# A third set of edges fetched row by row, by SyncE: a graph layer on one core

## The chip, the cores and the metric

The kernel runs on one core of a Trainium2 chip. A core has TensorE (PE, matrix products), VectorE (DVE), ScalarE (ACT), GpSimd (POOL) and SyncE (SP, which only issues transfers and waits). SP, ACT and POOL can issue transfers (DMAs) between HBM and the core's memory. The metric is the device time of one launch in microseconds (us), as the median of several runs.

## What is computed

The reference is one layer of a graph network on 50000 nodes of 160 features (64 scalars s and 32 vectors v of three components), with 1650000 edges sorted by their destination: 800000 random ones, the same turned round, and one from each node to itself. Each edge has four numbers e0 and e1 (three components).

```
ss, vv = s[src], v[src]
dot    = einsum('eui,ei->eu', vv, e1)
out0   = C0 * (ss*e0 @ W1 + dot*INV3 @ W2)
p3     = (ss @ W3)[:, :, None] * e1[:, None, :] * INV3
p4     = einsum('eui,uw->ewi', vv*e0, W4) * INV3
p5     = einsum('eui,uw->ewi', cross(vv, e1), W5) * INV6
m      = concat(out0, C1 * (p3 + p4 + p5))
m_agg  = segment_sum(m, dst)
h      = m_agg through Ws and Wv
out    = layernorm(x + x + relu(h))
```

All of it is linear in x[src] for given edge numbers. So the kernel first adds up x[src] times each of the four edge numbers over the edges of a destination (160 x 4 sums a node), and applies the products of the weights once per node.

## The kernel before, in words

**Units, pairs, stages.** The edges are worked in units of 128: one unit is one matmul `ps += ha.T @ xg` at line 502. `xg` holds the source rows of its 128 edges (128 x 160 f32); `ha` says, for four edge numbers and a window of 32 destination nodes, what each edge adds where. Six units make a group, two groups a pair (12 units, one PSUM tile `ps`), ten pairs a stage (120 units). There are some 104 stages. The loop over pairs begins at line 1002; in it a matmul is issued for each unit, and between them the program puts the other work: turning the sums and adding them into a ring of node sums (lines 518 and 527), making the next pair's `ha` (lines 474 and 477), blocks of 128 nodes finished by PE (line 822), DVE (lines 185 to 201) and ACT (line 195), their residual rows loaded (`xt`, line 765) and results sent (line 920).

**Where source rows come from.** GpSimd fetches most units with one indirect DMA each (`gather`, line 459), into a pool of four `xg` tiles of a pair each; so it can be up to four pairs ahead of PE. Two units in each stage of 120 are fetched otherwise: DVE makes a list of byte offsets (`list_rows`, lines 403 and 404), and ACT loads 32 of them at a time into registers (line 372) and issues one DMA of 640 bytes for each edge (line 376, 128 for a unit), into tiles `xscalar`. These rows have semaphores of their own; the matmul that reads the tile waits for the full count (line 505). That is the class `Fetcher` (line 351). The set of fetched units of a stage s is asked for from pair 4 of stage s - 1 to pair 4 of stage s, evenly by unit (`deal`, line 388): with two sets, one in the first half of this and one in the second. They stand at units 38 and 98 of the stage (line 357). Fetching runs in all stages but the first ones and the last ones (line 1026).

**SyncE's queue** carries, in the order of the program: the edges of the stage after next (`r`, `fd`, lines 270 and 276), the residual rows, the node rows and shares for a new part of the ring (`xr`, `sa`, line 798), the sends, and the packing. Packing takes the self edges out: in eleven packs of 128 rows of edges, DVE and ACT shift the edges together (lines 604 to 706) in a tile `prow`, and SyncE writes each row back with two DMAs (`store` and `put`, lines 715 to 740: one of 28 KB, one of 0.8 KB), 16 in a batch after one load of offsets (line 722), 17 batches in a pack. The next pack's first ACT operation (line 604) overwrites `prow` and waits for these stores.

**Order.** SP, PE, DVE and ACT run in the order in which the program writes their instructions (line 1000). Work of nodes is queued as tasks and worked off one step per unit (`work`, line 872); steps of a pack are spread evenly up to their due pair (line 1032). A send waits for DVE's result `o` (line 201); the residual rows of a block are waited for by DVE's `hot` (`lands`, line 466).

Of the kernel before, what the change touches and what calls it, by code (L numbers as in the profile page):

```python
# [77 lines left out]
KM = WS - 1  # L78
REST = 15
LEAD = 3  # L80
BY_SCALAR, BY_SYNC = 2, 0
FBEGIN, FWAIT = 4, 4

def plan(n_nodes, n_edges):
# [1132 lines left out]
```

## Time and profile before

| | us |
|---|---|
| median of 3 runs | 15476.25 (15474.15 to 15478.85) |
| profiled execution, its own time | 15480.47 |
| its span, first to last instruction | 15478.7 |

The profile shows one further execution. In its views PE, DVE, ACT and POOL are the engines; PEld is the loading of a matmul's weights; SPq, ACTq and POOLq are the queues of instructions that issue or wait, whose time is not counted as busy. `out<-in` names the tiles that an instruction writes and reads, L459 is a line of the kernel, x12 a count. "idle before, releaser" is the time in which an engine did nothing ahead of an instruction, and what ended it; "issue" means that it waited for nothing the profile shows. In a view of one line or tile the three numbers are the shortest, median and longest duration in ns, then first and last start.

### The profile page before, as it was taken

What the parts mean: (1) busy time and instruction counts of PE and PEld (TensorE: products, weight loads), DVE (VectorE), ACT (ScalarE), POOL (GpSimd) and SP (SyncE); (2) the same over time, 40 slices, a digit from 0 to 9 for tenths busy, and PEclk for the clock granted to TensorE, in tenths of its full rate; (3) what the DMA queues carried; (4) which work ended last, traced back from release to release, by engine and by line L of the source; (5) the groups of instructions that cost most, each with busy time, mean ns of one, the idle gap of its engine ahead of it and who ended that gap; (6) DMA issues with size and microseconds to landing.
All of it is one profiled execution on the core that took longest, in us unless ns stands there. A gap on an engine that the chain in (4) does not pass through costs nothing.

```text
span 15478.7 us, 148655 instructions
## 1 busy us (share of the span) xinstructions
PE 10475.4 (68%) x28971; PEld 6817.4 (44%) x28972; DVE 7640.9 (49%) x12532; ACT 171.6 (1%) x273; POOL 11680.1 (75%) x12331
## 2 busy tenths in 40 slices
PE   3466766667666666766666666667666666766666
PEld 3344444444444444444444444444444444444444
DVE  8455355445535543563455355445534553554333
ACT  0000000000000000000000000000000000000000
POOL 7777777777777777777777777777777777777777
PEclk6655555555555555555555555555555555555555
DMA  3333333333333333333333333333333333333333
GB/s 83 96 84 95 89 81 84 100 86 80 92 93 81 82 97 89 80 85 100 84 81 93 92 81 83 99 87 80 85 100 84 81 89 90 80 86 85 83 81 75
DMA packets 887906, 1345.20 MB, mean 87 GB/s; under 512 B 281438, under 2 KB 660450, under 8 KB 884310
## 3 DMA queue, kind: packets, MB, share of 16 engines
q0 software_dynamic: 591264, 1009.88, 27.6%
q1 hardware_dynamic: 242218, 308.07, 6.2%
q10 hardware_dynamic: 53488, 17.70, 0.6%
q14 instruction: 705, 5.78, 0.1%
q8 instruction: 231, 3.78, 0.1%
HBM read 1263.28 MB, written 71.42 MB: 86 GB/s over the span
## 4 chain that ended last, share of the span: by engine, by line
POOL 53%; issue 24%; DMA 16%; PE 6%; DVE 1%; POOLq 0%
POOL xg L459 53%; DMA xg<-in_x,si 16%; PE ps L502 5%; PE phb L822 1%; DVE ha L477 0%; DVE ring L527 0%; DVE sums L518 0%; DVE ring L813 0%; DVE hot L474 0%; DVE prow L688 0%; DVE xr L809 0%; DVE pri L683 0%; DVE marks L681 0%; DVE ring L524 0%; DVE ring L772 0%
## 5 line engine op out<-in xcount | busy, mean ns | idle before, releaser
L459 POOL DMA_INDIRECT xg<-in_x,si x12318 | 11676.6, 948 | 3777.4 <-issue 3517.7
L502 PE MATMUL ps<-xg,ha 128*128 128x160 f32 x24636 | 9735.6, 506 | 4990.9 <-DMA xg<-in_x,si 4453.7
L502 PEld LDWEIGHTS ps<-xg,ha 128*128 128x128 f32 x24636 | 5828.3, 293 | 8646.9 <-DMA xg<-in_x,si 7413.5
L518 DVE STREAM_TRANSPOSE sums<-ps 128x320 f32<-128x320 f32 x1044 | 535.5, 513 | 6834.6 <-PE ps L502 6820.7
L477 DVE TENSOR_TENSOR ha<-hot,pk 128x1536 f32<-128x1536 f32 x1044 | 1829.7, 1753 | 35.8
L822 PE MATMUL phb<-BWk,ring 128*128 128x160 f32 (+1 forms) x3910 | 1289.8, 428 | 0.0
L822 PEld LDWEIGHTS phb<-BWk,ring 128*128 128x128 f32 (+1 forms) x3910 | 1058.1, 304 | 0.1
L527 DVE TENSOR_TENSOR ring<-ring,sums 128x160 f32 x2087 | 683.1, 327 | 329.3 <-issue 190.7
L474 DVE TENSOR_TENSOR hot<-bank,rel 128x384 f32<-128x384 f32 x1044 | 572.4, 548 | 44.2 <-DMA xt<-in_x 42.4
L688 DVE COPY_PREDICATED prow<-marks,prow 128x2370 f32<-128x2370 int32 (+5 forms) x198 | 548.5, 2770 | 1.1
L813 DVE STREAM_TRANSPOSE ring<-xr 128x1280 f32<-128x1280 f32 x188 | 469.0, 2495 | 6.5
L688 DVE COPY_PREDICATED pra<-marks,pra 128x1580 f32<-128x1580 int32 (+5 forms) x198 | 377.0, 1904 | 0.0
L809 DVE TENSOR_TENSOR xr<-xr,bank 128x1280 f32<-128x1280 f32 x188 | 278.8, 1483 | 6.6 <-DVE bank L808 0.2
L185 DVE SCALAR_TENSOR_TENSOR y<-phb,xt 128x320 f32<-128x320 f32 x196 | 95.6, 488 | 308.7 <-PE phb L822 308.2
L195 ACT ACTIVATE rstd<-mv,eps_t 128x2 f32<-128x2 f32 x196 | 58.0, 296 | 14063.1 <-DVE mv L190 13240.1
L524 DVE TENSOR_TENSOR ring<-ring 128x196 f32<-128x196 f32 (+20 forms) x485 | 148.9, 372 | 1.8
L502 PE MATMUL ps<-xscalar,ha 128*128 128x160 f32 x408 | 146.8, 462 | 0.0
L201 DVE TENSOR_SCALAR o<-y,mv,rstd 128x160 f32<-128x160 f32 x391 | 131.7, 378 | 7.5
L685 DVE COPY_PREDICATED_SCALAR hit<-marks,none 128x395 int32 (+5 forms) x198 | 129.8, 655 | 7.0
L772 DVE MEMSET ring<- 128x1280 f32 (+1 forms) x98 | 119.3, 1218 | 22.6 <-issue 22.6
L189 DVE BATCH_NORM_STATS2 st<-y 128x6 f32<-128x160 f32 x391 | 121.6, 311 | 6.7
L686 DVE COPY_PREDICATED hit<-marks,pri 128x395 int32<-128x395 int32 (+5 forms) x198 | 118.1, 597 | 6.9
(351 smaller groups left out, 2061.2 us busy)
## 6 DMA issues: line engine op xcount, KB each, us to landing
xscalar<-in_x ACTq DMA_DIRECT2D x26112, 0.6 KB
xg<-in_x,si POOLq DMA_INDIRECT x12318
xr<-in_x SPq DMA_DIRECT2D x187, 640.0 KB
r<-edges SPq DMA_DIRECT2D x100, 384.0 KB
edges<-prow SPq DMA_DIRECT2D x1330, 27.8 KB
xt<-in_x SPq DMA_DIRECT2D x195, 160.0 KB
out<-o SPq DMA_DIRECT2D x195, 160.0 KB
pra<-in_attr SPq DMA_DIRECT2D x10, 2370.0 KB
```

The lines of the kernel that those rows point to most:

```text
L201: nc.vector.tensor_scalar(o[:n, i], y[:n, i], mv[:n, i, 0:1], rstd[:n, i:i + 1], op0=ALU.subtract, op1=ALU.mult)
L459: nc.gpsimd.indirect_dma_start(out=xg[:, j, :], out_offset=None, in_=x, in_offset=bass.IndirectOffsetOnAxis(ap=placed[0][:, u + j:u + j + ...
L474: idle[:] = [nc.vector.tensor_tensor(hot[:, :n], slotsP[:, 0:W].unsqueeze(1).to_broadcast([P, n, W]), rel[:, u:u + n].unsqueeze(2).to_broa ...
L477: nc.vector.tensor_tensor(ha[:, :n], hot[:, :n].unsqueeze(2).to_broadcast([P, n, NK, W]), pk[:, :, u:u + n].rearrange("p k u -> p u k").un ...
L502: mm = nc.tensor.matmul(ps[:, j // G, :], ha[:, j].rearrange("p k w -> p (k w)"), xr, start=j % G == 0, stop=j % G == G - 1)
L518: nc.vector.transpose(at[:, :ng], ps[:, :ng].rearrange("p g (b f) -> p g b f", f=FB))
L524: nc.vector.tensor_tensor(ring[k][:, b, :past], ring[k][:, b, :past], ring[k - 1][:, b, S:S + past], op=ALU.add)
L527: nc.vector.tensor_tensor(here, here, at[:, i], op=ALU.add)
L688: nc.vector.copy_predicated(what[:n, a:e], mi[:, r].unsqueeze(2).to_broadcast([n, e - a, what.shape[2]]), what[:n, a + d:e + d])
L809: nc.vector.tensor_tensor(xr[:, :nq], xr[:, :nq], sumP[:, :nq].unsqueeze(2).to_broadcast([P, nq, D]), op=ALU.mult)
L813: nc.vector.transpose(ring[k][:, :, c0:c0 + nq * W].rearrange("p b (w q) -> p q b w", q=nq), xr[:, :nq].rearrange("p q (b f) -> p q b f", ...
L822: wrote("misc", nc.tensor.matmul(ph[:nb], ring[k][:, i, c0:c0 + nb], BWk[:, i, :], start=i == 0, stop=i == ND - 1))
```

## The change

One constant: SyncE gets one set.

```
-BY_SCALAR, BY_SYNC = 2, 0
+BY_SCALAR, BY_SYNC = 2, 1
```

What follows from it in the program:

- The list of fetchers (line 394) has a second member: engine SP, a pool `sync` of two tiles (BY_SYNC + 1, line 245), eight semaphores, one set a stage. By line 357 its unit is ceil((4 + 10 + 4 - 10) x 12) + 8 = 104 of 120. Its rows are dealt over the same ten pairs, 128 in 120 units.
- SP's program gets, in each of these stages, four loads of 32 offsets and 128 DMAs of 640 bytes, in between what stands there already.
- GpSimd's program loses the gather of unit 104 in these stages: 12216 instead of 12318.
- PE's matmul of that unit reads `xsync` and waits for its semaphore.
- DVE's list is made for three units: one more operation at line 403, and 96 elements a partition instead of 64 at line 404.

## The prediction

> **What bounds the kernel now.** I read the page first: span, busy shares, the chain that ended last, the costliest groups.
>
> ```profile
> span 15478.7 us, 148655 instructions
> PE 10475.4 (68%) x28971; PEld 6817.4 (44%) x28972; DVE 7640.9 (49%) x12532; ACT 171.6 (1%) x273; POOL 11680.1 (75%) x12331
> ...
> POOL 53%; issue 24%; DMA 16%; PE 6%; DVE 1%; POOLq 0%
> ...
> L459 POOL DMA_INDIRECT xg<-in_x,si x12318 | 11676.6, 948 | 3777.4 <-issue 3517.7
> ```
>
> No engine is full, yet one explains the time. GpSimd issues 12318 gathers (line 459); their busy time and the idle time just before them are 11676.6 + 3777.4 = 15454.0 us, all of the span but 25 us. Of that idle time 3517.7 us is "issue": GpSimd waited for nothing that the profile shows. Next I asked the timeline what one gather takes, and whether anything else ever holds it up.
>
> ```profile
> 635.27 0.95 POOL L459 DMA_INDIRECT xg<-in_x,si  x1 [0.30 <-issue]
> 636.52 0.95 POOL L459 DMA_INDIRECT xg<-in_x,si  x1 [0.30 <-issue]
> ...
> 639.01 0.95 POOL L459 DMA_INDIRECT xg<-in_x,si  x1 [0.30 <-issue]
> 653.24 0.94 POOL L459 DMA_INDIRECT xg<-in_x,si  x1 [13.28 <-PE ps L502]
> 654.49 0.95 POOL L459 DMA_INDIRECT xg<-in_x,si  x1 [0.30 <-issue]
> ```
>
> A gather starts every 1.25 us: 0.95 us of work, 0.30 us between two. One real wait shows, 13.28 us at 640 us, and it matters below. Is 1.25 us a property of GpSimd, or does it give when SyncE and ScalarE issue beside it? I compared two stretches of 270 us, by busy time of line 459 (the columns: stretch, length, POOL busy, count, clock, DMA share, GB/s): one in which SyncE stores packed rows one by one while ScalarE fetches, one in which SyncE is almost quiet.
>
> ```profile
> 1410.00:1680.00 270.00, 204.46 (x216) 0.55 0.36 96
> 1740.00:2010.00 270.00, 204.21 (x216) 0.54 0.32 78
> ```
>
> 216 gathers in each, 1.25 us apiece, whatever the hardware queues do. So the kernel is bound by the number of gathers that GpSimd issues.
>
> **What the change removes.** ScalarE's fetched rows count the stages in which fetching runs. The views of its lines 376 and 372 give the register load, the issue and the load of 32 offsets (minimum, median and maximum in ns), the timeline an unbroken run of rows:
>
> ```profile
> L376 ACTq MOVE xscalar<-in_x x26112: 29/29/38, 245.2 to 15290.0; - x200
> L376 ACTq DMA_DIRECT2D xscalar<-in_x x26112: 227/228/1947, 245.3 to 15290.1; - x200
> ```
>
> ```profile
> L372 ACTq TENSOR_LOAD <-line x816: 2141/2298/6078, 242.9 to 15277.6; - x164
> ```
>
> ```profile
> 664.67 9.14 ACTq L376 DMA_DIRECT2D xscalar<-in_x  x29
> ```
>
> 26112 / 128 = 204 sets, two in a stage, so 102 stages; SyncE gets one set in each, the same condition. GpSimd loses 102 gathers: 102 x 1.25 = 127.5 us.
>
> **What it adds on SyncE.** 128 rows and four loads of offsets in a stage. The last row above has 29 rows in 9.14 us, 0.315 us each. The trace shows no such row on SyncE; its nearest row of the same kind is its own store (line 739, below), with 227 ns against 228 for the issue. So a stage adds 128 x 0.315 + 4 x 2.3 = 49.5 us of SyncE's time, and a stage lasts 118 x 1.25 = 147.5 us. What is free there? SyncE's own waits in one ordinary stage, 5000 to 5148 us:
>
> ```profile
> SPq L920 <- DVE center L321: 65.7, 1, 65.7
> SPq L920 <- DVE o L201: 61.3, 1, 61.3
> ```
>
> 127 us of 148: the rows fit into time that SyncE spends in front of line 920, the send of finished blocks. Queued behind the new wait for the list (line 372) are that engine's loads, sends and stores; but the list is asked for in the program at the pair whose DVE work makes it, where SyncE waits for the sends anyhow. The set is dealt until pair 4 of its stage (unit 48) and read at unit 104: 56 units, 70 us of slack, as with ScalarE's second set. The tile asked for was read two stages before, so its wait is nothing. PE's 102 sets of matmuls stay, with another operand. DVE gets one more operation of line 403 in a stage,
>
> ```profile
> L403 DVE TENSOR_SCALAR held<-r x198: 166/180/428, 705.6 to 15167.4; 128x32 f32<-128x32 f32 x198
> ```
>
> and a longer one at line 404; both lie in DVE's idle half (49% busy) and would be 102 x 0.18 = 18 us without that cover. Do ScalarE's rows suffer when SyncE issues beside them? In the stretch of stores from 1410 to 1680 us:
>
> ```profile
> L376 ACTq DMA_DIRECT2D xscalar<-in_x x487: 227/228/1175, 1417.6 to 1679.4; - x163
> ```
>
> The median stays at 228 ns, so I cost it at nothing; a doubled issue in all 128 rows would be 128 x 0.23 = 29 us a stage, beside 256 x 0.315 + 8 x 2.3 = 99 us of 147.5: it would still fit.
>
> **The one place without cover** is the first store of packed rows. SyncE's part, and its waits, from 407 to 628 us, then who waited from 560 to 720 us:
>
> ```profile
> L739 SPq DMA_DIRECT2D edges<-prow x136: 223/227/2102, 407.7 to 626.9; - x136
> L739 SPq DMA_DIRECT2D selves<-mine x136: 223/227/363, 408.1 to 627.3; - x136
> ```
>
> ```profile
> SPq L739 <- DMA edges<-prow: 62.7, 93, 3.0
> SPq L739 <- DMA selves<-mine: 13.4, 53, 0.3
> ```
>
> ```profile
> ACT prow L604 <- DMA edges<-prow: 122.8, 1, 122.8
> ...
> DVE hot L474 <- DMA xt<-in_x: 42.4, 1, 42.4
> ...
> POOL xg L459 <- PE ps L502: 13.9, 3, 13.3
> ```
>
> SyncE is late here. DVE waits 42.4 us for a load of nodes queued behind the stores, ScalarE 122.8 us for the stores' end, DVE for ScalarE, PE for DVE; GpSimd, up to four buffers ahead, loses the 13.28 us seen above. Any delay of the stores' end goes straight into that loss. In the changed order 101 rows and four loads of the second set stand among these 272 stores (five rows and a load just ahead of the first), five to seven rows between two batches of 16. They take 101 x 0.315 + 4 x 2.3 = 41 us of issue. Upper bound: 41 us, all added. Lower bound: 0, since SyncE waits 76 us in 146 places for its own transfers, and rows issued meanwhile cost nothing; below nothing it can't be, as nothing is taken off this queue. I take 12 us, nearer to the waits' row: a batch's rows take some 2 us of issue, against 76 / 17 = 4.5 us of waiting per batch, and are hidden; what is left is the rows' time in the transfer queue, by ScalarE's queue (packets, MB, share)
>
> ```profile
> q10 hardware_dynamic: 53488, 17.70, 0.6%
> ```
>
> 0.006 x 16 x 15478.7 / 26112 = 0.057 us a row, 101 of them 5.8 us, and some 2 us (an estimate) for each of the three loads inside the stretch, which come together with rows (2.3 + 2 us, about a batch's wait). Also, the two sets used before this wait (units 104 of stages 2 and 3) gain nothing: GpSimd merely waits 2.5 us longer. In the later ten packs the stores' end is not waited for: in the second one the last stores are issued at 1683 us and ScalarE overwrites the rows at 1875 us:
>
> ```profile
> 1683.70 0.23 SPq L739 DMA_DIRECT2D selves<-mine  x1
> ```
>
> ```profile
> 1874.80 2.30 ACT L604 CAST prow<-pri 128x1185 f32<-128x1185 int32 x1 [27.64 <-PE ps L502]
> ```
>
> 191 us of room against some tens of delay.
>
> **Sum.** -127.5 + 2.5 + 12 = -113 us. The profiled execution took 15480.47 us (1.8 around its span), so 15367.5; it lies 4.2 us over the median of the runs, so I forecast 15363 for the median.
>
> [...] The GpSimd rows above are the bound, at 1.25 us for each issue. [...]
>
> **Rivals.**
> 1. *The first pack costs more.* The 41 us are added whole, and ScalarE, catching up after it, falls up to as far behind again: -127.5 + 2.5 + 41 to twice 41, so 15392 to 15433. For it: SyncE's queue has no free time from 407 to 628 us. Against: the 76 us of waits.
> 2. *The transfer is the bound, not the issue.* If the gathers' pace came from the DMA engines, each fetched row would give its time back: 15476. For it: DMA holds 16% of the chain. Against: 216 gathers in both stretches, at 96 and 78 GB/s.
> 3. *Slower: SyncE can't issue a set in a stage.* SyncE's 147.5 us less 20 of other work and 9.2 of loads leave 118 us, 0.92 us a row; above that each stage waits for its rows. Its stores, with their waits, go at (627.3 - 407.7) / 272 = 0.81 us; at 1.0 us a row a stage takes 128 + 29 = 157 us in place of 147.5, 102 of them 970 us more: 16446. Against: the row's 0.315 us on ScalarE, three times faster than the limit.
>
> That the change doesn't do what it says is excluded: 102 gathers fewer stand in the built program, and PE reads 102 of SyncE's tiles.
>
> **How the numbers follow.** Forecast 0.79: 15363, with its own range from 15347 (nothing lost in the first pack: -127.5 + 2.5, 15351, and the 4 us by which runs scatter) to 15392. Rival 1 0.07, rival 2 0.06, rival 3 0.08. The range, 15345 to 15400, holds the forecast and the near part of rival 1. A measurement here can tell about 0.2%, 31 us. Faster: 0.79 + 0.07 = 0.86; same 0.06; slower 0.08.
>
> **What would show it.** GpSimd's count falls to 12216 and its interval stays at 1.25 us, or the sum's first term is wrong. The wait near 640 us grows from 13.3 to about 28 us (13.3 + 2.5 + 12). Line 376 on SyncE shows 13056 issues near 228 ns. PE shows no new long waits before a matmul on xsync. The forecast is wrong if the interval rises past 1.263 us (12216 x 0.0104 = 127 us), or if GpSimd waits for PE in many stages.

## The result, and the profile after

| | before | after |
|---|---|---|
| median of 15 runs of each, us | 15474.18 (15469.4 to 15479.1) | 15444.51 (15439.69 to 15449.57) |
| profiled execution, its span, us | 15478.7 | 15438.1 |

The ratio of after to before is 0.9981, with an interval of 0.9973 to 0.9989: 30 us won, 0.2%, where 113 were forecast and the range ended at 15400. The profiled execution of before lay some 6 us above its median and that of after some 4 us below its own, so the two profiles are 40.6 us apart, and the budget below has to explain those.

From the page of after: span, engines, the queue of SyncE (q1) and that of ScalarE (q10), the chain that ended last, and the group of the gathers.

```profile
span 15438.1 us, 175175 instructions
...
q1 hardware_dynamic: 268330, 316.48, 6.6%
q10 hardware_dynamic: 53488, 17.70, 0.6%
...
POOL 51%; issue 21%; DMA 19%; PE 4%; DVE 1%; SPq 0%; POOLq 0%; DVEq 0%
...
L459 POOL DMA_INDIRECT xg<-in_x,si x12216 | 11581.5, 948 | 3831.6 <-issue 3491.8
```

The count is 12216 as forecast and the mean of one is 948 ns in both kernels. But the idle time ahead of the gathers rose from 3777.4 to 3831.6 us although there are 102 fewer of them, and only part of it is "issue". What the rest is, the waits of GpSimd over the whole span say (total in us, times, longest). Before:

```profile
POOL xg L459 <- issue: 3517.7, 11532, 1.3
POOL xg L459 <- PE ps L502: 203.3, 623, 13.3
POOL xg L459 <- DMA xg<-in_x,si: 44.7, 134, 1.0
```

After:

```profile
POOL xg L459 <- issue: 3491.8, 11413, 2.0
POOL xg L459 <- PE ps L502: 185.1, 437, 33.7
POOL xg L459 <- DMA xg<-in_x,si: 140.4, 328, 1.7
```

Each gather has some 0.30 us of idle time before it anyway, whatever is named as its releaser. So each row is read by what it holds over 0.30 us a time. Waits for PE: 203.3 - 623 x 0.30 = 16.4 us before, 185.1 - 437 x 0.30 = 54.0 after, so +37.6. Waits for the transfer of an earlier gather: 44.7 - 134 x 0.30 = 4.5 before, 140.4 - 328 x 0.30 = 42.0 after, so +37.5. "Issue": 0.3050 us a time before, 0.3059 after, so 11413 x 0.0009 = some +10. With -127.5 for the gathers that went, the sum is -42 us, against 40.6 measured between the spans. Two costs are to be explained, of about 37 and 48 us.

**The first: PE's waits at the first pack.** Who waited from 560 to 760 us in after:

```profile
ACT prow L604 <- DMA edges<-prow: 142.6, 1, 142.6
...
DVE hot L474 <- DMA xt<-in_x: 68.1, 1, 68.1
PE ps L502 <- DVE ha L477: 58.1, 1, 58.1
DVE hit L625 <- ACT marks L624: 53.6, 3, 36.7
...
POOL xg L459 <- PE ps L502: 48.3, 2, 33.7
```

GpSimd's 13.3 us became 48.3, in two waits, one of 33.7 and the other of 14.6 us. DVE's wait for the nodes queued behind the stores grew by 68.1 - 42.4 = 26 us. The stores themselves, from 400 to 700 us in after:

```profile
L739 SPq DMA_DIRECT2D edges<-prow x136: 223/228/1047, 412.2 to 662.5; - x136
L739 SPq DMA_DIRECT2D selves<-mine x136: 223/228/1199, 412.5 to 662.8; - x136
```

They end at 662.8 us instead of 627.3, 35.5 us later. The busy time of the gathers up to 760 us (columns as in the prediction) shows the loss by the count. Before, then after:

```profile
0.00:760.00 760.00, 560.34 (x586) 0.66 0.35 89
```

```profile
0.00:760.00 760.00, 529.29 (x554) 0.65 0.31 85
```

32 gathers fewer, of which two were taken out: GpSimd stands 30 x 1.25 = 37.5 us behind.

**The second: gathers that come in late, everywhere.** SyncE's rows go out as fast as ScalarE's:

```profile
L376 SPq MOVE xsync<-in_x x13056: 29/29/39, 244.7 to 15225.3; - x198
L376 SPq DMA_DIRECT2D xsync<-in_x x13056: 224/228/9388, 244.7 to 15225.3; - x198
```

PE waits for none of them. But where both engines issue rows at once, as in this stretch of after (SyncE, then ScalarE),

```profile
6789.81 18.36 SPq L376 DMA_DIRECT2D xsync<-in_x  x39
```

```profile
6790.04 18.54 ACTq L376 DMA_DIRECT2D xscalar<-in_x  x49
```

GpSimd is held up for a moment, and what ends its wait is the transfer of an earlier gather:

```profile
6808.54 0.95 POOL L459 DMA_INDIRECT xg<-in_x,si  x1 [0.30 <-issue]
6810.39 0.94 POOL L459 DMA_INDIRECT xg<-in_x,si  x1 [0.91 <-DMA xg<-in_x,si]
6812.07 0.94 POOL L459 DMA_INDIRECT xg<-in_x,si  x1 [0.73 <-DMA xg<-in_x,si]
6813.72 0.94 POOL L459 DMA_INDIRECT xg<-in_x,si  x1 [0.70 <-DMA xg<-in_x,si]
```

The rows hardly slow each other's issue: each of these two runs has a load of 32 offsets of some 2.3 us in it, and from row to row ScalarE takes 0.342 us on average with a row of SyncE's within 0.4 us, and 0.345 without; SyncE takes 0.358 with one of ScalarE's and 0.355 without (steps under 1.5 us). But three gathers lose 0.61 + 0.43 + 0.40 us here.

The trace's packet records tell where. A gather is recorded as 16 packets each of 640, 4480 and 4 bytes (before, 591264 packets for 12318 gathers, 48 each) and raises its semaphore in 16 steps; a sixteenth of it, eight rows, is called a share here. A fetched row is one packet of 640 bytes and one of 4: in after SyncE's queue has 13056 more of each, for 13056 rows. In eight of the gathers from 6802 to 6818 us, one of the 16 packets of 4480 bytes took 0.75 to 1.17 us; from 6710 to 6730 us, 99 in 100 took 0.38 us or less. One share of sixteen is late, and the wait for a gather ends with its last share, as the next paragraph shows.

One late share doesn't hold GpSimd yet. The records of the semaphores (the counters that a transfer raises when it lands) show that the gathers go round eight of them, and that each waits for the one eight before it, issued some 10 us earlier. The gather at 6810.39 us started 0.26 us after the last share of that earlier gather had landed, at 6810.14; its other 15 shares had landed by 6802.36. The next two gathers show the same, 0.26 us behind a share that came over 8 us after the other 15. So a queue is worked off: the packets of the rows go on until 6816.6 us, 8 us after the last of them was issued, and GpSimd stands still here where this queue outlasts eight gathers. From 760 to 15300 us, 12 gathers before and 312 after had a last share that landed more than 7 us behind the middle one.

The same records show the order in that queue. From 6806.1 to 6816.7 us the packets of 640 and 4 bytes of SyncE's queue and of ScalarE's, and the gathers' six late ones (0.76 to 1.17 us), stand one behind the other, none overlapping the next by more than 6 ns: no row's packet runs beside a late one. No view names a transfer engine. That one engine carries a row, and that the rows of both queues and the late shares meet on the same one, is the author's inference from this place; the expectations below take it as given.

### The profile page after: what moved, and what is told of

The parts are those of the page before. It is cut to its first block, busy times and chain, and to the rows that moved or that the text cites. A ratio compares the mean times of both kernels' runs of the same rounds, so it can differ in the third digit from the quotient of the medians.

```text
span 15438.1 us, 175175 instructions
## 1 busy us (share of the span) xinstructions
PE 10171.0 (66%) x28971; PEld 6746.8 (44%) x28972; DVE 7652.8 (50%) x12634; ACT 171.5 (1%) x273; POOL 11585.0 (75%) x12229
## 4 chain that ended last, share of the span: by engine, by line
POOL 51%; issue 21%; DMA 19%; PE 4%; DVE 1%; SPq 0%; POOLq 0%; DVEq 0%
POOL xg L459 51%; DMA xg<-in_x,si 18%; PE ps L502 3%; DMA selves<-mine 1%; PE phb L822 0%; DVE ha L477 0%; SPq L739 0%; DVE prow L688 0%; DVE ring L527 0%; SPq L376 0%; DMA xt<-in_x 0%; DVE sums L518 0%; DVE hot L474 0%; DVE ring L813 0%; DVE xr L809 0%
## 5 line engine op out<-in xcount | busy, mean ns | idle before, releaser
L459 POOL DMA_INDIRECT xg<-in_x,si x12216 | 11581.5, 948 | 3831.6 <-issue 3491.8
L502 PE MATMUL ps<-xg,ha 128*128 128x160 f32 x24432 | 9418.3, 500 | 5253.2 <-DMA xg<-in_x,si 4659.5
L502 PEld LDWEIGHTS ps<-xg,ha 128*128 128x128 f32 x24432 | 5765.7, 292 | 8675.4 <-DMA xg<-in_x,si 7382.9
L822 PE MATMUL phb<-BWk,ring 128*128 128x160 f32 (+1 forms) x3910 | 1250.3, 417 | 0.0
L822 PEld LDWEIGHTS phb<-BWk,ring 128*128 128x128 f32 (+1 forms) x3910 | 1020.3, 294 | 0.0
L474 DVE TENSOR_TENSOR hot<-bank,rel 128x384 f32<-128x384 f32 x1044 | 573.1, 549 | 69.9 <-DMA xt<-in_x 68.1
```

Source lines behind the costliest of these rows:

```text
L459: nc.gpsimd.indirect_dma_start(out=xg[:, j, :], out_offset=None, in_=x, in_offset=bass.IndirectOffsetOnAxis(ap=placed[0][:, u + j:u + j + ...
L474: idle[:] = [nc.vector.tensor_tensor(hot[:, :n], slotsP[:, 0:W].unsqueeze(1).to_broadcast([P, n, W]), rel[:, u:u + n].unsqueeze(2).to_broa ...
L502: mm = nc.tensor.matmul(ps[:, j // G, :], ha[:, j].rearrange("p k w -> p (k w)"), xr, start=j % G == 0, stop=j % G == G - 1)
L822: wrote("misc", nc.tensor.matmul(ph[:nb], ring[k][:, i, c0:c0 + nb], BWk[:, i, :], start=i == 0, stop=i == ND - 1))
```

## The experiments

**Theory 1**: both costs come from the added rows, late stores in the first pack and late gathers in the rest; **theory 1a**: by their number, not their bytes. Its rivals put the loss elsewhere: into the gap that the missing gather leaves in the order of PE's pairs (A), into transfers of ScalarE and GpSimd that have moved against the stores (B), into SyncE's rows alone without ScalarE's (C), or, for the first pack, into the rows' transfers and not SyncE's time (E). D is a cost of the paced versions: loads and stores that come late. The expectations state them with their numbers.

**The first four runs** come from a chip where the kernel before itself took 20491.12 us. There ScalarE is slow, and not GpSimd the bound, so they don't answer the question.

Gathers removed (unit 104 reads a tile of zeros; these edges are left out of the sums):

```diff
-BY_SCALAR, BY_SYNC = 2, 1
+BY_SCALAR, BY_SYNC = 2, 0
@@ gather
+                if rows[j] is None and u + j == 104 and 1 < s < NSC - 1:
+                    rows[j] = nothing, None, None, None
```

> The kernel before, with the gather of unit 104 left out in the same 102 stages and nothing fetched in its place; its matmul reads a tile of zeros, so those edges are left out of the sums. Theory 1 (the interval of 1.25 us per gather is GpSimd's own): 102 x 1.25 = 127.5 us less, of which 2.5 us are lost in the first pack: 15474 - 125 = 15349, GpSimd's interval unchanged. Rival A (pairs with two fetched units wait for PE): clearly less, about half, 15400 to 15420.

Rows added (all gathers kept, SyncE's rows fetched as well):

```diff
-                if rows[j] is None:
+                kept = rows[j] is None
+                if kept:
                     rows[j] = xg[:, j, :], None, None, None
+                if kept or u + j == 104:
                     nc.gpsimd.indirect_dma_start(
```

> The changed kernel, but GpSimd gathers unit 104 as well (into its place in the gathered tile, which nothing reads), so that only the price of SyncE's rows is left, against the kernel before. The changed kernel's profile puts 38 us more than before into the first 760 us and some 48 us into gathers later on that start late, 1.5 to 2.7 us after the one before. Theory 1 (the two losses are the price of the rows, whatever GpSimd does): 15474 + 86 = 15560, from 15545 to 15575. Rival A (the late gathers come from PE or from the pairs with two fetched units, so they go when the gather is kept): only the first pack is left, 15474 + 38 = 15512.

Late start (SyncE's sets begin only after the first pack):

```diff
+FIRST = 4
@@ list_rows
-                f.prepare(s, line[:, i], at, u0 + at)
+                if f.et != ET.SP or s > FIRST:
+                    f.prepare(s, line[:, i], at, u0 + at)
@@ loop over pairs
-                        f.begin(0 < s < NSC - 2)
+                        f.begin((0 if f.et != ET.SP else FIRST - 1) < s < NSC - 2)
```

> The changed kernel, but SyncE's fetching begins three stages later, for the set of stage 5, after the first pack's stores. 99 gathers fewer than before instead of 102. Theory 1 (the first pack's loss comes from rows queued among the stores on SyncE): the stores from 412 to 663 us end near 627 again, GpSimd's wait near 640 us is back at 13.3 us, and the time is 15444 - 38 + 3.75 = 15410. Rival B (the stores end late because the transfers of ScalarE and GpSimd have moved against them): the stores still end past 650 us and the time stays near 15445.

One set each:

```diff
-BY_SCALAR, BY_SYNC = 2, 1
+BY_SCALAR, BY_SYNC = 1, 1
```

> The changed kernel with one set for ScalarE and one for SyncE instead of two and one: as many gathers (12318) and as many fetched rows as before, but from two queues. Theory 1 (gathers start late where the rows of both queues together load one transfer engine): half of ScalarE's rows are gone, so the late gathers go too, and only the first pack's loss is left: 15474 + 38 = 15512, GpSimd's waits for transfers near 4 us over its usual interval as before. Rival C (two hardware queues that issue at the same time disturb GpSimd or each other, whatever the sum of rows): the late gathers stay, 15474 + 38 + 30 to 48 = 15540 to 15560.

Measured on that chip: gathers removed 20360.39 us (ratio 0.9929, 0.9906 to 0.9952), rows added 21107.81 (1.0296, 1.027 to 1.0322), late start 20935.52 (1.0225, 1.0202 to 1.0248), one set each 19685.72 (0.961, 0.9586 to 0.9635). Waits of the first of them:

```profile
ACT rstd L195 <- issue: 18146.0, 176, 150.4
...
DVE rstd L199 <- ACT rstd L195: 6435.3, 133, 74.6
POOL xg L461 <- PE ps L506: 4027.1, 354, 46.5
```

DVE waits 6435 us for ScalarE, 4.3 us on the usual chip, and GpSimd waits for PE 4027 us. ScalarE's 22 rows in one unbroken run took 23.78 us there, 30 of them 11.99 us on the usual chip, each with one load of offsets. With ScalarE the bound, a set taken from it helps and rows added beside its own cost more. Why that chip's ScalarE was slow isn't settled. All later runs come from chips where the kernel before took 15475 to 15485 us.

**1. The gathers removed, again.**

> The kernel before, with the gather of unit 104 left out in the same 102 stages and nothing fetched in its place; its matmul reads a tile of zeros, so those edges are left out of the sums. It is run again because the first four runs came from a chip on which the kernel before took 20491 us. Where the kernel before takes some 15475 us: theory 1 (the interval of 1.25 us per gather is GpSimd's own) gives 102 x 1.25 = 127.5 us less, 2.5 us of it lost in the first pack: ratio 0.9919. Rival A (pairs with two fetched units wait for PE): clearly less, about half, ratio 0.995 to 0.997.

15363.14 us against 15484.4: ratio 0.9922 (0.9906 to 0.9939), -121 us. Waits of GpSimd:

```profile
POOL xg L461 <- PE ps L506: 198.0, 594, 17.3
POOL xg L461 <- DMA xg<-in_x,si: 46.9, 142, 1.4
```

Over the usual 0.30 us, 19.8 and 4.3 us, against before's 16.4 and 4.5. Nothing new is waited for, so A is out: the missing gather costs PE nothing. The first term of the forecast's sum holds.

**2. The rows added, again**, on top of all gathers.

> The changed kernel, but GpSimd gathers unit 104 as well (nothing reads it), so that only the price of SyncE's rows is left; run again for a chip on which the kernel before takes some 15480 us. Without the gathers and without the rows the time was 15363 against 15484, so removing is worth 121 us; the changed kernel gained 30, so the rows should cost some 91. Theory 1 (the first pack's loss and the late gathers are the price of the rows, whatever GpSimd does): 91 us more than before, ratio 1.0059. Rival A (the late gathers come with the pairs that have two fetched units, and go when the gather is kept): the first pack's 38 us alone, ratio 1.0025.

15569.51 us against 15476.57: ratio 1.0061 (1.0046 to 1.0077), +93 us. Its waits:

```profile
POOL xg L461 <- PE ps L504: 178.5, 431, 31.5
POOL xg L461 <- DMA xg<-in_x,si: 132.5, 301, 1.8
```

49.2 and 42.2 us over the usual, as in after. -121 + 93 = -28, the change's -30: the two halves add up, and the whole loss is what the rows cost.

**3. The late start, again.** It leaves SyncE's rows out of the first pack; three sets of 102 aren't fetched, so 99 x 1.25 = 124 us are to be won.

> The changed kernel, but SyncE's fetching begins three stages later, for the set of stage 5, after the first pack's stores; 99 gathers fewer than before instead of 102. Run again as above. Theory 1 (the first pack's loss comes from rows queued among the stores on SyncE): the stores end near 627 us again instead of 663, GpSimd's wait near 640 us is back at 13.3 us, and the ratio to before is 0.9981 - (38 - 3.75) / 15474 = 0.9959. Rival B (the stores end late because ScalarE's and GpSimd's transfers have moved against them): they still end past 650 us, ratio 0.998.

15406.55 us: ratio 0.9954 (0.994 to 0.9967), -70 us. Its stores from 400 to 700 us, then GpSimd's waits:

```profile
L741 SPq DMA_DIRECT2D edges<-prow x136: 223/228/2060, 406.9 to 627.1; - x136
```

```profile
POOL xg L461 <- PE ps L504: 148.5, 434, 14.1
POOL xg L461 <- DMA xg<-in_x,si: 132.5, 310, 2.7
```

The stores end at 627 us again, the longest wait for PE is 14.1 us, and 40 us of the loss are gone. B is out. The 39.5 us of late gathers stay: the two costs are separate.

**4. One set each for ScalarE and SyncE**: as many rows and gathers as before, split over two queues.

> The changed kernel with one set for ScalarE and one for SyncE instead of two and one: as many gathers (12318) and as many fetched rows as before, from two queues. Run again as above. Theory 1 (gathers start late where the rows of both queues together load one transfer engine): with half of ScalarE's rows gone the late gathers go too, and only the first pack's 38 us are left: ratio 1.0025, and GpSimd's waits for transfers come near those of before (44.7 us by the page). Rival C (rows from SyncE's queue delay the gathers whatever the sum of rows, for instance because they share it with stores and loads): the late gathers stay, 38 + 30 to 48 us: ratio 1.0044 to 1.0056, and the waits for transfers near 140 us.

15495.38 us: ratio 1.0012 (1.0003 to 1.0021), +19 us. Waits:

```profile
POOL xg L459 <- PE ps L502: 187.5, 517, 29.6
POOL xg L459 <- DMA xg<-in_x,si: 58.3, 177, 1.7
```

The late gathers are gone: 58.3 - 177 x 0.30 = 5.2 us, though SyncE fetches as many rows as in after. Last shares more than 7 us behind are 17 here, against 312 in after. So C is out: the sum of both engines' rows makes gathers late. The first pack still loses, but less than I expected: its stores end at 643.7 us, and waits for PE hold 32.4 us over the usual where after has 54.0. ScalarE's own rows there are halved.

**5. The late start, paced.** In experiment 3, SyncE has its rows issued in bursts, whenever it comes out of a wait. Here the first row after each pair's nodes waits for DVE's `hot` of that pair, which spreads them.

```diff
                     row.then_inc(sem, 16)
+                    if self.et == ET.SP and paced:
+                        tc.add_manual_dep(row.ins, paced.pop().ins.name, LANDED)
@@ loop over pairs, beside experiment 3's edit
                     has[p + 1] = spread(placed[s1], (g1 - s1 * SG) * G, ng1 * G)
+                    paced[:] = idle[:]
```

> The late start, and in each pair the first of SyncE's rows after the making of that pair's operand also waits for it (VectorE's line 474), so that SyncE issues some 13 rows a pair of 15 us instead of all rows between two sends at 0.318 us each. Theory 1 (a gather starts late when ScalarE and SyncE both issue rows at full rate, six or seven in the 1.25 us of one gather): with four to five rows in that time most of the 48 us of late gathers go, so 30 to 45 us less than the late start: ratio 0.993 to 0.994. Rival C (it is the rows as such, not their rate): no change against the late start, ratio 0.996. Rival D (SyncE, now held at each pair, brings its loads and stores late): slower than the late start.

15378.65 us: ratio 0.9937 (0.9924 to 0.9951), -98 us, 28 better than unpaced, with the same rows.

```profile
POOL xg L463 <- DMA xg<-in_x,si: 74.3, 202, 1.4
```

13.7 us over the usual instead of 39.5, and 140 last shares more than 7 us behind instead of 334. What makes gathers late is rows of both engines in the same microseconds. D is out: pacing made nothing slower on balance.

**6. SyncE's rows of 64 bytes** instead of 640 (nine tenths of those rows' features are left out of the sums).

```diff
-                    row = self.engine.dma_start(tile_[0].bitcast(U8)[p:p + 1],
-                                                xbytes[ds(self.asked[e], 4 * D)].rearrange("(o f) -> o f", o=1))
+                    m = 64 if self.et == ET.SP else 4 * D
+                    row = self.engine.dma_start(tile_[0].bitcast(U8)[p:p + 1, :m],
+                                                xbytes[ds(self.asked[e], m)].rearrange("(o f) -> o f", o=1))
```

> The changed kernel, but each of SyncE's rows is 64 bytes instead of 640 (the rest of its tile is set to zero by VectorE, so 9 tenths of those features are left out of the sums). It asks what of a row costs: its number or its bytes. Theory 1a (each row costs by being a transfer: an issue on SyncE and a descriptor on the one engine that carries it): nothing changes, stores end near 663 us, ratio 0.998 as for the changed kernel. Theory 1b (it costs by its bytes): the late gathers mostly go and the stores end clearly earlier, ratio 0.994 to 0.995.

15445.69 us against 15478.09: ratio 0.998 (0.9971 to 0.9989), the same as after.

```profile
POOL xg L462 <- PE ps L505: 195.0, 473, 32.0
POOL xg L462 <- DMA xg<-in_x,si: 137.4, 304, 2.3
```

Both costs are there in full (53.1 and 46.2 us over the usual). Between 64 and 640 bytes it is the number of rows, not their bytes.

**7. ScalarE paced as well.**

```diff
-                    if self.et == ET.SP and paced:
-                        tc.add_manual_dep(row.ins, paced.pop().ins.name, LANDED)
+                    if self.et in paced:
+                        tc.add_manual_dep(row.ins, paced.pop(self.et).ins.name, LANDED)
@@ loop over pairs
-                    paced[:] = idle[:]
+                    paced.update({f.et: idle[0] for f in fetchers})
```

> Late start and pacing for SyncE as in the run before (ratio 0.9937), and ScalarE's rows paced in the same way, by VectorE's line 474 of each pair. Theory 1 (gathers start late when rows come in bursts of both queues): ScalarE too now issues some 26 rows a pair instead of 47 when it is free, the rest of the late gathers goes, 10 to 25 us less: ratio 0.992 to 0.993. Rival D (ScalarE, held at each pair, brings its casts and square roots late, and VectorE waits for them): slower than with SyncE paced alone, over 0.994.

15366.99 us against 15478.09: ratio 0.9929 (0.9916 to 0.9943), -111 us, the best version of all. That this is close to what was forecast for the change itself is chance: it is another kernel, with 99 sets and two paced streams.

```profile
POOL xg L463 <- DMA xg<-in_x,si: 57.7, 174, 2.0
```

5.5 us over the usual, near before's level, with 18 last shares more than 7 us behind. Single packets of 4480 bytes over 0.75 us are as many here as in after, 2169 and 2230 from 760 us on (1562 before): it is the length of the queue that counts, not that a share is late.

**8. A pause among the first pack's stores, without rows.** The kernel before, with the 16 offsets of each batch loaded one at a time.

```diff
-                _, spot = nc.values_load_multi_w_load_instructions(
-                    spots[0:1, i0:i0 + 2 * ni], engines=[ET.SP], min_val=0,
...
+                spot, step = [], 2 * ni if c else 1
+                for k in range(i0, i0 + 2 * ni, step):
+                    spot += nc.values_load_multi_w_load_instructions(
+                        spots[0:1, k:k + step], engines=[ET.SP], min_val=0,
```

> The kernel before, with no rows on SyncE at all; in the first pack alone the 16 store offsets of a batch are loaded by 16 loads of one number instead of one load of 16, so that SyncE pauses longer between two batches of stores and issues no further transfer in the pause. By the two loads seen so far (1.24 us for 16 numbers, 2.3 us for 32) one number should take some 0.2 us or more, 16 of them 3.5 us or more: 2 to 3 us longer a pause, 17 batches, 35 to 50 us, as long as the rows' issue (41 us) in the changed kernel. Theory 1 (it is SyncE's time that delays the stores' end; the waits do not take it up): the stores end 30 us or more later than 627 us and the time is 25 to 40 us over before, ratio 1.0016 to 1.0026. Rival E (it is the rows' transfers that delay the stores, a mere pause is taken up by the waits for the stores' landing, as the prediction had it): the stores end within 10 us of 627 us, ratio 1.000 to 1.0006.

15510.03 us against 15475.52: ratio 1.0022 (1.0012 to 1.0032), +34.5 us. The loads of offsets from 400 to 700 us, before and then here; then the stores here, and the waits that SyncE has among them from 400 to 670 us:

```profile
L722 SPq TENSOR_LOAD <-spots x17: 1165/1233/1514, 406.3 to 619.7; - x17
```

```profile
L724 SPq TENSOR_LOAD <-spots x270: 260/268/784, 404.3 to 651.8; - x135
...
L741 SPq DMA_DIRECT2D selves<-mine x136: 223/228/976, 409.7 to 657.4; - x136
```

```profile
SPq L741 <- DMA edges<-prow: 22.8, 22, 4.3
...
SPq L741 <- DMA selves<-mine: 3.1, 12, 0.3
```

By the medians, 270 x 0.268 - 17 x 1.233 = 51 us of issue more, and the stores end 30 us later. The waits fell from 76.1 to 25.9 us, by 50, and yet 30 us came through. So E is out in its full form: the waits aren't free time. Where they go shows in the stores' own issues, added up over the 272 records of the timeline: 65.2 us before, 97.0 here. So part of the waiting moved from ahead of the issues into them, 31.8 us. Waits and issues together fell from 141.3 to 122.9 us: 18 us of a pause of 51 are taken up by them.

The records of landings say what these waits were. Each store of 28 KB is one packet, of 1.05 us in the median, and in a batch each store waits for the one four such stores before it. In the kernel before, one store landed every 1.38 us (median). Steps of over 2.4 us are 6 there and hold 30 us beyond that pace; in this run they are 16 and hold 61, in after 15 and 57, in experiment 4 15 and 43. That is 31, 27 and 13 us more, most of what the stores' ends moved (30, 35.5 and 16). So SyncE's waits were mostly the stores' own transfers, one after another at a steady pace, and a pause lets that sequence stop.

## Why the prediction was wrong

**The first term was right.** 102 gathers at 1.25 us were -127.5 (with 2.5 us given back in the first pack), -121 alone on the chip. The added rows cost 93, of which the late gathers are some 48; a loss in the first pack came from a mere pause too (34.5 us, experiment 8).

**The step that failed first: "I take 12 us"** for the first pack. It was about 37. Two reasons stood for 12: that a batch's rows, some 2 us of issue, are hidden in 4.5 us of waits per batch, and that only their transfers' 5.8 us and three loads remain. In after SyncE's waits among the stores are

```profile
SPq L739 <- DMA edges<-prow: 53.4, 39, 7.1
SPq L739 <- DMA selves<-mine: 5.7, 23, 0.3
```

59.1 us instead of 76.1, but the issues of the 272 stores add up to 85.1 us instead of 65.2. Together 144.2 against 141.3: "rows issued meanwhile cost nothing" did not hold, nothing was taken up, and the rows' time came on top, near the upper bound of 41 that the prediction had worked out and left. One batch of after shows how:

```profile
444.41 1.92 SPq L376 DMA_DIRECT2D xsync<-in_x  x6
447.73 0.29 SPq L739 DMA_DIRECT2D edges<-prow  x1
...
450.13 0.23 SPq L739 DMA_DIRECT2D selves<-mine  x1
456.54 0.23 SPq L739 DMA_DIRECT2D edges<-prow  x1
```

After the rows eight stores go out at once, then SyncE waits 6.2 us for the first of them, whose semaphore tells of the landing at 456.52 us: a wait is not removed, it is moved behind the burst. How much comes through depends on what runs beside it: a pause of 51 us without more rows moved the stores' end by 30 (experiment 8), the rows beside one set of ScalarE's by 16 (experiment 4), the same rows beside two sets by 35.5, of 41 us of issue. That these rows and the stores meet in a transfer engine is the author's inference; no view names the engine, and it was not tested apart. In the batch shown, the store issued at 447.73 us began its transfer only at 453.89, 3.6 us after the last row's; why it took so long stays open. Rival 1 named the place and the price of 41, but what it added, ScalarE falling as far behind again, did not come: GpSimd lost about as much as the stores' end moved.

**The step that failed second: the gathers' pace "whatever the hardware queues do".** It was taken as unchanged and cost some 48 us (37.5 in waits for the gathers' transfers, 10 in "issue"). The view behind it could not have shown this. Two stretches of 270 us with 216 gathers each are equal to one gather in 216, 0.46%, and that is 72 us of the whole kernel. In after, the same stretches read

```profile
1410.00:1680.00 270.00, 204.03 (x216) 0.56 0.36 105
1740.00:2010.00 270.00, 202.97 (x216) 0.57 0.33 89
```

216 again, though in the second one the waits for transfers hold 1.6 us over the usual. Only a long stretch shows it by count: from 760 to 15300 us GpSimd issued 11607 gathers before and 11570 after, 37 fewer in the same time, or 46 us. Nor was the case of the change in it: ScalarE's rows beside SyncE's stores, not two streams of rows. GpSimd's row of waits for its own transfers, 44.7 us in 134 times before, would have said that gathers were already late now and then.

**The other parts.** SyncE's rows took 228 ns in the median as ScalarE's do, and 0.47 us with a load of offsets in the stretch quoted, against the 0.92 that fit, and PE waited for none of them, so rival 3 (a stage too short for them) is out. Rival 2 (the transfer is the bound, no gain at all) is out as put, since the gathers alone gave 121 us; its idea, that the transfers take some back, is what happened (37.5 us in GpSimd's waits for its own), by the number of rows and not by their bytes (experiment 6). The forecast said that it would be wrong if GpSimd waited for PE in many stages: after the first 760 us it doesn't. The interval's mean from 760 to 15300 us, 14540 / 11570 = 1.257 us (before 1.253), stays under 1.263, so this sign was set too wide to catch a loss of 46 us. Neither sign named the waits for the gathers' own transfers.

## What to carry to other kernels

Before work is moved from the engine that bounds a kernel to one that idles, count the transfers that it adds to those under way in the same microseconds, by number and not by bytes (rows of 64 and of 640 bytes cost the same here), ask how far one late share may lag before an issuer has to wait (eight gathers here, some 10 us), and look for the stretch where the receiving queue is late already: there, take its waits as spent until a run shows otherwise (here 76.1 us of waits took up 18 of a pause of 51). A row of waits is a better witness than a count of instructions in a stretch, whose resolution, one instruction, must be set against the whole kernel. Here starting late (40 us) and pacing both row streams (41 us more) brought back nearly all that the plain change had lost.

## What the runs showed of the hardware

- A DMA of a single row costs its issuing engine some 0.315 us with the register move, on SyncE as on ScalarE (medians of 29 and 228 ns at 640 bytes, 29 and 228 at 64; from row to row 318 ns on ScalarE and 322 on SyncE, medians of after). Its transfer is recorded as one packet of 640 bytes and one of 4.
- GpSimd's gathers here go round eight semaphores: each waits for the last of the 16 shares of the gather eight before it. Before, 1624 last shares landed over 4 us behind the middle one and 12 over 7 us, and such waits held 4.5 us over the usual; after, 312 landed over 7 us behind, and the waits held 42.0.
- SyncE's stores of 28 KB, one packet of 1.05 us each, landed one every 1.38 us in the first pack; the time that SyncE waited for them was not free for other work: a pause of 51 us moved their end by 30 (experiment 8).
- SyncE's register loads in these runs: 268 ns for one offset, 1233 ns for sixteen (medians).
- One chip ran the kernel before in 20491 us instead of 15476. With the gathers removed, an unbroken run of 22 of ScalarE's rows and a load took 23.78 us there, while over the whole run its moves and issues had the usual medians, 29 and 228 ns (longest 1676 and 1678; 38 and 1947 on the usual chip); nothing in these traces says why.
